# Projections and output projection in two pieces on TensorE, the time step in four, and new places for some tasks

## The chip, the cores and the metric

The kernel runs on one core of one Trainium2 chip. The metric is device microseconds of one execution. The names of the engines in the profile: PE is TensorE's matmul, PEld its weight load, DVE is VectorE, ACT is ScalarE, POOL is GpSimd, SP is SyncE, which issues the DMAs here.

## The reference

A decoder layer on x of shape (16, 256, 512), in three parts, each with a residual and a layer norm:

```
x = layernorm(x + mamba(x))            # selective state space, DI = 1024 channels, 16 states
x = layernorm(x + cross_attn(x, ctx))  # 16 heads of 16; channels and positions change their roles
x = layernorm(x + ffn(x))              # quantized weights (-1, 0, 1) and activations (8 bit)

# mamba
hs, gate = x @ W_in_states.T, x @ W_in_gates.T            # (256, 1024) each
hs = silu(causal_conv4(hs) + conv_b)
dt = softplus(hs @ W_dt.T @ W_dtproj.T + b)               # W_dt: to 128
h[l] = exp(A * dt[l]) * h[l-1] + dt[l] * B[l] * hs[l]     # 16 states for each channel
y = (sum_n h * C + hs * D) * silu(gate)
out = y @ W_out.T
```

## The kernel before

**Stages.** Each of the 16 batches goes through four functions: `prep` (state projection, convolution, time step, B and C, softplus), `scan` (gate projection, recurrence, gated output), `attn` (output projection, first norm, keys, queries, values, scores, second norm) and `ffn`. They don't run one after the other: stages of up to five batches are in flight together.

**Tasks and places.** The functions emit no instructions. They make tasks by `task(t, engine, us, fn, after, take, free)`: `t` is the place, counted in slots, with 32 slots for each batch (NSL); `us` is what the planner takes the task to last; `after` names the tasks that have to be done; `take` and `free` name buffers of rings (`Hold`). At the end `run()` plays all of this through in a planner's time: whenever an engine is idle there, it starts the ready task with the lowest `t`, not more than AHEAD = 12.29 slots past the first task that hasn't begun, and emits its instructions. A task's end is known to others HOP = 0.2 us later, and 0.3 us later where PE did it. So the order on each engine's queue is fixed by the planner, and a task is never interrupted. On the chip each queue runs in that order, with semaphores between the engines.

**Constants.** The places are constants at the head of the file: a batch b starts at T = 32 b; PREP, TSP, BCP, SOFT for `prep`; GATE, SUMP, WEIGHP for `scan`; OUT0 and OUT1 for the two halves of the output projection, KP and QP for keys and queries, NORM for the second norm, FFN, FSTEP, FUP, FDN for the feed-forward part, WS0 and WQ0 for the passes over the feed-forward weights at the start.

**Rings.** Buffers are few. TensorE's results go to PSUM: five banks (`ps`) are shared by projections, scores, sums and the rest; two more hold decays (`dA`) and one the attention output (`av`). There are seven `h` buffers (the states of 32 channels and four state groups), two `z`, two `win`, one `wr` (used in turn by the step weights and by the context), one `wout`, three `xres`.

**The long TensorE tasks.** Each is one task of 3.45 us in the planner:
- `project` (L491): 8 fp32 matmuls, that is two channel tiles of four k steps, into the two halves of a PSUM bank. `prep` makes four of them per batch, `scan` four more (gates). After one in `prep` come ACT (L510), three DVE steps for each half (L517), ACT (L530) and DVE (L520); after one in `scan` ACT (L641) and DVE (L638).
- the time step (L544): 8 matmuls, one chain of accumulation. For batch 0 it is cut in four already.
- the output projection (L736): four matmuls of 512 columns, one chain of accumulation, for each half of the channels and each row tile; then DVE adds to the residual (L740).

**The other TensorE tasks** are short: scores (L830), values (L896), state sums (L694 and L697, 2.45 us in the planner), key and query projection (L763), feed-forward (L1013, L1086), transposes.

**The recurrence.** For each tile d of 128 channels and each of four groups, POOL makes the product dt*hs*B (L233, `h<-bcr,dtr`), ACT the decays (L668), DVE two scans (L672), POOL the product with C (L233, `h<-h,bcr`). Then PE sums over the states (L697) and frees four `h` buffers, and DVE multiplies by the gate (L705). The loads `dtr<-dtd` (L654) feed it.

Of the kernel before, what the change touches and what calls it, by code (L numbers as in the profile page):

```python
# [20 lines left out]
P = 128  # L21
L = 256
# [3 lines left out]
NDT = DI // P  # L26
# [18 lines left out]
SOFT = -7.09  # L45
SSTEP = 9.0
VUNITS = 24
GATE = -0.34
OUT0 = 25.01
OUT1 = 34.11  # L50
PSTEP = 2.02
TSP = 15.44
BCP = 9.29
KP = 34.45
QP = 37.76
VP = -3.68
SUMP = 0.16
WEIGHP = 1.88
FSTEP = 0.74
FUP = -0.18  # L60
BACK = 0.59

SHIFT = [(0, 0, 0, 0, 0, 0)] * 16
# [3 lines left out]
SLAG = 7.79  # L67
GSTEP = 3.93
SCAN = -0.29
NORM = 81.05  # L70
FFN = 98.49
WQ = 3.57
WQ0 = 21.99
WS = 0.66
WS0 = 14.23
AHEAD = 12.29
HOP = 0.2
RINGS = {
# [8 lines left out]
def decoder_kernel(ctx, tc, x, xT, ctx_in, mask, winT, wdtT, wbcT, wdpT, woutT, dvec, wqkvT, bqk, bv, wguT, wdnT, out):  # L87
    nc = tc.nc
# [55 lines left out]
    def task(t, eng, us, fn, after=(), take=(), free=(), kb=0):  # L144
        if any(h.tag == "ps" for h in free) and eng in ("DVE", "ACT"):
            t -= BACK
        k = Task()
        k.t, k.i, k.eng, k.us, k.fn, k.take, k.free, k.kb = t, len(tasks), eng, us, fn, take, free, kb
        k.then, k.begun = [], False
        k.left = len(after)  # L150
        for p in after:
            p.then.append(k)
        for h in take:
            h.first = k
        for h in free:
            h.users += 1
        tasks.append(k)
        return k

    def led(h, *after):  # L160

        return tuple(after) + ((h.first,) if h.first is not None else ())
# [90 lines left out]
    for i in range(RINGS["dA"]):  # L253

        t = ps.tile([P, 2, L], F32, tag=f"dA{i}", name=f"dA{i}", bufs=1)
# [7 lines left out]
    def cut(t, a, b):  # L263
        return t.rearrange("p (a b) -> p a b", a=a, b=b)
# [28 lines left out]
    for g in range(NB4):  # L293
# [7 lines left out]
        for n in range(1, NB4):  # L301
            t = cut(free["tmp"][n % 2][:, : NDT * NS // NB4], NDT, NS // NB4)
# [180 lines left out]
        h = Hold(tag)  # L483
        return h, dma(t, lambda: nc.sync.dma_start(out=cut(h.t, 4, 2 * P), in_=winT[:, :, c0 : c0 + 2 * P]), (), (h,), (), 512)

    def project(ps_t, hx, hw):

        xt, ws = cut(hx.t, 4, L), cut(hw.t, 4, 2 * P)
        for i in range(2):
            for k in range(4):  # L490
                nc.tensor.matmul(ps_t[:, i * L : (i + 1) * L], ws[:, k, i * P : (i + 1) * P], xt[:, k, :], start=k == 0, stop=k == 3)  # L491


    def prep(b):
        st = S[b]
        T = b * NSL + SHIFT[b][0]
        hx, t_x = st["xT"] = load_x(T + PREP - 3, b)
# [6 lines left out]
        for d0 in range(0, NDT, 2):  # L504
            t = T + PREP + PSTEP * d0
            hw, t_w = load_win(t - 5, d0 * P) if b else load_win(T + PREP - 3 + 0.1 * d0, d0 * P, "h")
            pb, z = Hold("ps"), Hold("tmp")

            def first(i, pb=pb, z=z, d0=d0):
                nc.scalar.activation(  # L510
                    z.t[:, i * L : (i + 1) * L], pb.t[:, i * L : (i + 1) * L], AF.Identity, bias=cw[:, d0 + i, 4:5], scale=cw[:, d0 + i, 3:4]
                )

            def conv(i, j, pb=pb, z=z, d0=d0):
                s = 3 - j
                zi = z.t[:, i * L + s : (i + 1) * L]
                nc.vector.scalar_tensor_tensor(zi, pb.t[:, i * L : (i + 1) * L - s], cw[:, d0 + i, j : j + 1], zi, ALU.mult, ALU.add)  # L517

            def silu(pb=pb, z=z, d0=d0):
                nc.vector.scalar_tensor_tensor(u2_of(d0), cut(pb.t, 2, L), 1.0, cut(z.t, 2, L), ALU.add, ALU.mult)  # L520

            uh = (st["u"][d0 // 4],) if d0 % 4 == 0 else ()
            m = task(t, "PE", 3.45, lambda pb=pb, hw=hw: project(pb.t, hx, hw), led(st["u"][d0 // 4], t_x, t_w), (pb, z) + uh, (hx, hw))
            ends = []
            for i in range(2):
                k = task(t, "ACT", 0.52, lambda i=i, f=first: f(i), (m,))
                for j in (2, 1, 0):
                    k = task(t, "DVE", 0.42, lambda i=i, j=j, f=conv: f(i, j), (k,))
                ends.append(k)
            k = task(t, "ACT", 0.53, lambda pb=pb, z=z: nc.scalar.activation(pb.t, z.t, AF.Tanh), tuple(ends))  # L530
            st["t_u"].append(task(t, "DVE", 0.61, silu, (k,), (), (pb, z)))
        U = tuple(st["t_u"])


        t = T + PREP + TSP
        hw, hts, hbc = Hold("wr"), Hold("ts"), Hold("bc")
        hwd = Hold("win" if b else "h")
        t_wdt = dma(t - 3 if b else T + PREP - 2, lambda: nc.sync.dma_start(out=cut(hwd.t, NDT, P), in_=wdtT), (), (hwd,), (), 512)
        t_wdp = dma(t - 1 if b else T + PREP - 1.9, lambda: nc.sync.dma_start(out=hw.t, in_=wdpT), (), (hw,), (), 512)
        pts, p2, p3, hp2 = Hold("ps"), Hold("ps"), Hold("ps"), Hold("o")  # L540

        def time_step(d0, n):
            for d in range(d0, d0 + n):
                nc.tensor.matmul(pts.t[:, :L], cut(hwd.t, NDT, P)[:, d, :], u_of(d), start=d == 0, stop=d == NDT - 1)  # L544
# [12 lines left out]
            src = st["bcd"][o : o + NS, :].rearrange("(n j) l -> n (j l)", n=NB4)  # L557
            nc.sync.dma_start(out=h.t, in_=src[None].broadcast_to([DB, NB4, NS // NB4 * L]))

        if b:  # L560
            m = task(t, "PE", 3.45, lambda: time_step(0, NDT), U + (t_wdt,), (pts, hts), (hwd,))
        else:
            for i in range(4):
                m = task(
                    t, "PE", 0.87, lambda i=i: time_step(2 * i, 2), (U[i], m if i else t_wdt), (pts, hts) if i == 0 else (), (hwd,)
                )
        t_ts = task(t, "ACT", 0.37, lambda: nc.scalar.copy(hts.t, pts.t[:, :L]), (m,), (), (pts,))
        m = task(T + PREP + BCP, "PE", 1.1, bc, U + (t_wbc,), (p2, hbc, hp2))
        m = task(T + PREP + BCP, "ACT", 0.37, lambda: nc.scalar.copy(hp2.t, p2.t[:, :L]), (m,), (), (p2,))
        m = task(T + PREP + BCP, "PE", 0.5, lambda: nc.tensor.matmul(p3.t[:32, :L], sel4, hp2.t, start=True, stop=True), (m,), (p3,), (hp2,))  # L570
        m = task(T + PREP + BCP, "ACT", 0.36, lambda: nc.scalar.copy(hbc.t, p3.t[:32, :L]), (m,), (), (p3,))
        m = dma(t + 0.5, bc_store, (m,), (), (hbc,), 32)
# [6 lines left out]
        for hf in range(2):  # L579
            t = T + SOFT + SSTEP * hf  # L580
# [17 lines left out]
            for i, (d, h) in enumerate(zip(ds, hs)):  # L598
# [10 lines left out]
                m = task(t + 1 + i, "POOL", 1.25, times, (t_s,))  # L609
# [4 lines left out]
    def scan(b):  # L614
        st = S[b]
# [14 lines left out]
        hx, t_x = st["xT"]  # L630
        st["z"], st["t_z"] = [], []
        for i in range(4):
            d0, t = 2 * i, T + 8 * i + GATE
            hw, t_w = load_win(t - 5, DI + d0 * P)
            pb, z = Hold("ps"), Hold("z")

            def silu(pb=pb, z=z):
                nc.vector.scalar_tensor_tensor(z.t, z.t, 1.0, pb.t, ALU.add, ALU.mult)  # L638

            m = task(t, "PE", 3.45, lambda pb=pb, hw=hw: project(pb.t, hx, hw), (t_x, t_w), (pb, z), (hx, hw))  # L640
            m = task(t, "ACT", 0.53, lambda pb=pb, z=z: nc.scalar.activation(z.t, pb.t, AF.Tanh, scale=0.5), (m,))  # L641
            st["z"].append(z)
            st["t_z"].append(task(t, "DVE", 0.61, silu, (m,), (), (pb,)))
        for d in range(NDT):
            hs, ws = [], []
            for g in range(NB4):
                k = NB4 * d + g
                t = T + k - SCAN
# [28 lines left out]
                f = dma(t - 4, fetch, (st["t_dt"][d // 2],), (hd,), (), 256)  # L677
# [10 lines left out]
            pb = Hold("ps")  # L688
# [18 lines left out]
            m = task(T + 4 * d + 4 + SUMP, "PE", 2.45, sums, tuple(ws), (pb,), tuple(hs))  # L707
# [3 lines left out]
    def attn(b):  # L711
        st = S[b]
# [5 lines left out]
        U = T + SHIFT[b][2]  # L718
# [6 lines left out]
        for hf in range(2):  # L725
            hw = Hold("wout")
            wo = lambda hw=hw: cut(hw.t, 4, H)
            t_w = dma(U + (OUT1 if hf else OUT0) - 8, lambda hf=hf, wo=wo: nc.sync.dma_start(out=wo(), in_=woutT[:, 4 * hf : 4 * hf + 4, :]), (), (hw,), (), 1024)
            for lt in range(2):
                t = U + (OUT1 if hf else OUT0) + 0.7 * lt  # L730
                pb = Hold("ps")

                def mult(hf=hf, lt=lt, pb=pb, wo=wo):
                    for i in range(4):
                        u = cut(st["u"][hf].t, 4, L)
                        nc.tensor.matmul(pb.t, u[:, i, lt * P : (lt + 1) * P], wo()[:, i, :], start=i == 0, stop=i == 3)  # L736

                def add(lt=lt, pb=pb):

                    nc.vector.scalar_tensor_tensor(x1()[:, lt, :], pb.t, 0.5, x1()[:, lt, :], ALU.mult, ALU.add)  # L740

                m = task(t, "PE", 3.45, mult, (t_w,) + tuple(st["t_y"][4 * hf : 4 * hf + 4]), (pb,), (hw, st["u"][hf]))
                adds[lt].append(task(t, "DVE", 0.61, add, (m, t_x1), (), (pb,)))
        t_n1 = layernorm(U + OUT1 + 1.3, hr, adds)

# [3 lines left out]
        t = T + OUT1 - 1  # L749
# [43 lines left out]
        for s in range(4):  # L793
            t = T + att + SLAG + VP + 0.7 * s
            pb = Hold("ps")
# [9 lines left out]
            m = task(t, "PE", 1.0, mult, (t_c, t_wqkv, t_bv) + (tuple(S[b - 1]["t_av"]) if b else ()), (pb,), (hc,))  # L805
# [122 lines left out]
        t = T + NORM + SHIFT[b][4]  # L928
# [11 lines left out]
        m = task(t, "DVE", 0.5, lambda: nc.vector.reciprocal(hrc.t, hsm.t), (t_sm,), (hrc,), (hsm,))  # L940
# [236 lines left out]
```

## Time and profile before

| | us |
|---|---|
| runs: median of 3 (lowest, highest) | 3010.79 (3008.86, 3011.28) |
| profiled execution, its own time | 3007.98 |
| its span, first to last instruction | 3005.8 |
| busy: PE, PEld | 2650.5, 1319.4 |
| busy: DVE, ACT, POOL | 2674.1, 2334.0, 2596.5 |
| mean granted TensorE clock | 0.965 |

A line of the groups or of the timeline names the line of the kernel, the engine, the operation and the tiles. Two matmul records stand for one fp32 matmul. In the list of waits, "POOL h L233 <- PE bank L697" says that POOL's instruction of L233 waited for the matmul of L697, with the us in total, the number of times and the longest. A row of the windows gives, for a stretch of time, the busy us of PE, PEld, DVE, ACT and POOL with the number of instructions in brackets, then the granted clock, the share of the DMA engines and GB/s.

### The profile page before, as it was taken

The page shows a single profiled execution, that of the slowest core. Times are in us where ns is not written, and L with a number is a line of the kernel's source. Part 1 is how long each engine was busy: PE and PEld are TensorE (multiplying, and loading weights), DVE is VectorE, ACT ScalarE, POOL GpSimd, SP SyncE. Part 2 cuts the span into 40 slices and gives each one's busy share as a digit, 9 for nine tenths or more (in the row PEclk, how much of TensorE's full clock was granted, in tenths as well). Part 3 has the DMA queues.
Part 4 walks back from the last instruction along what each step waited for, and adds up shares of the span by engine and source line. Part 5 has one row for each costly group of instructions (what it writes and reads, how often), then busy time and mean ns, then how long its engine had stood idle before and what let it go on. Part 6 is the DMA issues. An engine that isn't in the chain of part 4 may idle for free.

```text
span 3005.8 us, 51881 instructions
## 1 busy us (share of the span) xinstructions
PE 2650.5 (88%) x17514; PEld 1319.4 (44%) x17514; DVE 2674.1 (89%) x4043; ACT 2334.0 (78%) x4731; POOL 2596.5 (86%) x1435
## 2 busy tenths in 40 slices
PE   6567888999989999898999989899998999999995
PEld 4333443454545445444444544444353544434333
DVE  6969888999989999898999989899999989999873
ACT  4787978787787878778787877878788787888674
POOL 3899999999898999989899998989989899999311
PEclk9787999999999999999999999999999999999998
DMA  6695776566465665746665574656646566564432
GB/s 215 222 305 182 233 224 205 188 199 206 143 218 182 204 195 171 224 138 214 193 200 186 168 224 150 216 189 196 189 157 226 165 203 193 187 203 147 125 98 71
DMA packets 363250, 567.46 MB, mean 189 GB/s; under 512 B 47316, under 2 KB 200024, under 8 KB 358888
## 3 DMA queue, kind: packets, MB, share of 16 engines
q1 hardware_dynamic: 362984, 564.16, 58.2%
q8 instruction: 137, 2.24, 0.3%
q14 instruction: 129, 1.06, 0.1%
HBM read 449.61 MB, written 114.43 MB: 188 GB/s over the span
## 4 chain that ended last, share of the span: by engine, by line
POOL 28%; PE 27%; DVE 16%; ACT 13%; issue 10%; DMA 5%; SPq 1%; POOLq 0%; ACTq 0%; DVEq 0%
POOL h L233 23%; DVE h L672 7%; PE bank L491 6%; ACT pT L889 4%; PE bank L697 4%; DVE mx L845 4%; PE av L896 3%; PE bank L830 3%; ACT dA L668 3%; PE bank L1013 3%; PE bank L763 2%; PE bank L799 2%; DMA dtr<-dtd 2%; ACT xres L469 1%; POOL s L233 1%
## 5 line engine op out<-in xcount | busy, mean ns | idle before, releaser
L672 DVE TENSOR_TENSOR_SCAN h<-dA,h 128x512 f32<-128x512 f32 x1024 | 1223.3, 1208 | 83.0 <-POOL h L233 41.2
L233 POOL TENSOR_TENSOR h<-h,bcr 128x1024 f32<-128x1024 f32 x512 | 1207.9, 2363 | 95.7 <-DVE h L672 92.9
L233 POOL TENSOR_TENSOR h<-bcr,dtr 128x1024 f32<-128x1024 f32 x500 | 1177.7, 2363 | 69.9 <-PE bank L697 63.4
L668 ACT ACTIVATE dA<-dtr,A 128x255 f32<-128x255 f32 x2048 | 963.9, 475 | 297.1 <-DVE h L672 255.6
L830 PE MATMUL bank<-qk 108*128 108x512 bf16 x2003 | 616.3, 385 | 78.9 <-DVE mx L845 44.7
L845 DVE TENSOR_REDUCE mx<-bank 128x1 f32<-128x512 f32 x1004 | 655.1, 675 | 25.8 <-PE bank L830 25.6
L889 ACT ACTIVATE pT<-bank 128x512 f32<-128x512 f32 x999 | 566.6, 590 | 119.1 <-PE bank L830 113.9
L491 PE MATMUL bank<-xT,win 128*128 128x256 f32 x1984 | 454.5, 382 | 20.4 <-DVE u L520 7.8
L896 PE MATMUL av<-pT,vaug 128*32 128x256 f32 x4096 | 336.2, 397 | 106.6 <-ACT pT L889 104.5
L491 PEld LDWEIGHTS bank<-xT,win 128*128 128x128 f32 x1984 | 377.2, 192 | 83.8 <-DVE u L520 9.5
L830 PEld LDWEIGHTS <-qk 108*128 108x128 bf16 x2048 | 179.7, 98 | 392.2 <-issue 264.2
L697 PE MATMUL bank<-h,sel 128*32 128x256 f32 x4096 | 262.0, 399 | 49.0 <-POOL h L233 48.9
L1013 PE MATMUL bank<-fw,xqT 128*128 128x512 fp8e4 x976 | 248.5, 381 | 12.5 <-DVE hq L1023 4.0
L896 PEld LDWEIGHTS av<-pT,vaug 128*32 128x32 f32 x4096 | 88.8, 109 | 356.8 <-ACT pT L889 277.9
L736 PE MATMUL bank<-wout,u 128*128 128x512 f32 x512 | 231.0, 595 | 4.9 <-DVE u L705 4.4
L697 PEld LDWEIGHTS bank<-h,sel 128*32 128x32 f32 x4096 | 124.1, 114 | 180.9 <-POOL h L233 72.2
L517 DVE SCALAR_TENSOR_TENSOR tmp<-bank,cw,tmp 128x254 f32<-128x254 f32 (+2 forms) x384 | 165.1, 468 | 7.8 <-ACT tmp L510 7.7
L1013 PEld LDWEIGHTS <-xqT 128*128 128x128 bf16 x1024 | 96.3, 98 | 151.4 <-issue 57.6
L736 PEld LDWEIGHTS bank<-wout,u 128*128 128x128 f32 x512 | 96.0, 190 | 108.5 <-issue 94.4
L1086 PE MATMUL bank<-fw,s 128*128 128x512 fp8e4 x496 | 127.0, 380 | 1.8 <-ACT s L1077 1.1
L233 POOL TENSOR_TENSOR s<-s,u 128x512 f32<-128x512 f32 x64 | 80.7, 1272 | 39.9 <-ACT s L595 39.9
L705 DVE TENSOR_TENSOR u<-bank,z 128x256 f32<-128x256 f32 x128 | 52.8, 413 | 60.9 <-PE bank L697 60.8
(157 smaller groups left out, 2961.7 us busy)
## 6 DMA issues: line engine op xcount, KB each, us to landing
dtr<-dtd SPq DMA_DIRECT2D x512, 256.0 KB
win<-in_winT SPq DMA_DIRECT2D x124, 512.0 KB
qk<-sqk SPq DMA_DIRECT2D x128, 384.0 KB
dtd<-s SPq DMA_DIRECT2D x64, 512.0 KB
wout<-in_woutT SPq DMA_DIRECT2D x32, 1024.0 KB
fw<-gu_q SPq DMA_DIRECT2D x64, 512.0 KB
sqk<-qf SPq DMA_DIRECT2D x64, 384.0 KB
bcr<-bcd SPq DMA_DIRECT2D x32, 512.0 KB
```

The source lines that it names most:

```text
L233: return nc.gpsimd.tensor_tensor(out, a, b, ALU.mult)
L491: nc.tensor.matmul(ps_t[:, i * L : (i + 1) * L], ws[:, k, i * P : (i + 1) * P], xt[:, k, :], start=k == 0, stop=k == 3)
L517: nc.vector.scalar_tensor_tensor(zi, pb.t[:, i * L : (i + 1) * L - s], cw[:, d0 + i, j : j + 1], zi, ALU.mult, ALU.add)
L668: nc.scalar.activation(ha.t[:, i, 1:], hd.t[:, 1:L], AF.Exp, scale=A[:, d, g, j : j + 1])
L672: nc.vector.tensor_tensor_scan(seg, ha.t.rearrange("p n l -> p (n l)"), seg, 0.0, ALU.mult, ALU.add)
L697: m = nc.tensor.matmul(pb.t[DB * g : DB * g + DB, :L], sel, cut(hs[g].t, J, L)[:, j, :], start=False, stop=j == J - 1, tile_position=(0, D ...
L736: nc.tensor.matmul(pb.t, u[:, i, lt * P : (lt + 1) * P], wo()[:, i, :], start=i == 0, stop=i == 3)
L830: nc.tensor.matmul(pb.t, qk()[:, j, side, c * P : (c + 1) * P], qk()[:, j, 1 - side, :], start=True, stop=True)
L845: task(t, "DVE", 0.62, lambda pb=pb, c=c, j=j: nc.vector.tensor_reduce(mx()[:, j, c : c + 1], pb.t, AX.X, ALU.max), (m,), (), (pb,))
L889: V["x"] = nc.scalar.activation(hp.t[:, j * H : (j + 1) * H], pb.t, AF.Exp, scale=DSC)
L896: i = nc.tensor.matmul(hav.t[32 * k : 32 * k + 32, :], vaug_f[:, c, c0 : c0 + 32], hp.t[:, j * H + h * L : j * H + (h + 1) * L], start=c == 0,
L1013: nc.tensor.matmul(pb.t, xqT()[:, i, t * P : (t + 1) * P], wu()[:, k, i, :], start=i == 0, stop=i == 3)
```

## The change

`project` makes two tasks of 1.73 us now, one for each channel tile, the second after the first. The output projection becomes two tasks of two matmuls each; the cut lies inside its chain of accumulation. The time step of every batch is cut in four tasks of two matmuls, as it was for batch 0. What follows them waits for the last piece. Nine places are changed.

```diff
-GATE = -0.34
-OUT0 = 25.01
-OUT1 = 34.11
+GATE = -1.46
+OUT0 = 24.55
+OUT1 = 33.92
-BCP = 9.29
-KP = 34.45
+BCP = 9.42
+KP = 33.05
-FSTEP = 0.74
-FUP = -0.18
+FSTEP = 0.66
+FUP = -0.8
-NORM = 81.05
+NORM = 82.79
-WS0 = 14.23
+WS0 = 12.95
...
-    def project(ps_t, hx, hw):
-
-        xt, ws = cut(hx.t, 4, L), cut(hw.t, 4, 2 * P)
-        for i in range(2):
+    def project(t, pb, hx, hw, need, got):
+
+        def mult(i):
+            xt, ws = cut(hx.t, 4, L), cut(hw.t, 4, 2 * P)
             for k in range(4):
-                nc.tensor.matmul(ps_t[:, i * L : (i + 1) * L], ws[:, k, i * P : (i + 1) * P], xt[:, k, :], start=k == 0, stop=k == 3)
+                nc.tensor.matmul(pb.t[:, i * L : (i + 1) * L], ws[:, k, i * P : (i + 1) * P], xt[:, k, :], start=k == 0, stop=k == 3)
+
+        m = task(t, "PE", 1.73, lambda: mult(0), need, got, (hx, hw))
+        return task(t, "PE", 1.73, lambda: mult(1), (m,), (), (hx, hw))
...
-        if b:
-            m = task(t, "PE", 3.45, lambda: time_step(0, NDT), U + (t_wdt,), (pts, hts), (hwd,))
-        else:
-            for i in range(4):
-                m = task(
-                    t, "PE", 0.87, lambda i=i: time_step(2 * i, 2), (U[i], m if i else t_wdt), (pts, hts) if i == 0 else (), (hwd,)
-                )
+        for i in range(4):
+            m = task(
+                t, "PE", 0.87, lambda i=i: time_step(2 * i, 2), (U if b else U[i : i + 1]) + (m if i else t_wdt,), (pts, hts) if i == 0 else (), (hwd,)
+            )
...
-                def mult(hf=hf, lt=lt, pb=pb, wo=wo):
-                    for i in range(4):
+                def mult(i0, hf=hf, lt=lt, pb=pb, wo=wo):
+                    for i in (i0, i0 + 1):
...
-                m = task(t, "PE", 3.45, mult, (t_w,) + tuple(st["t_y"][4 * hf : 4 * hf + 4]), (pb,), (hw, st["u"][hf]))
+                m = task(t, "PE", 1.73, lambda f=mult: f(0), (t_w,) + tuple(st["t_y"][4 * hf : 4 * hf + 4]), (pb,), (hw, st["u"][hf]))
+                m = task(t, "PE", 1.73, lambda f=mult: f(2), (m,), (), (hw, st["u"][hf]))
```

More of the change, by code (lines that the diff above doesn't have):

```diff
@@ L522, in prep @@
             uh = (st["u"][d0 // 4],) if d0 % 4 == 0 else ()
-            m = task(t, "PE", 3.45, lambda pb=pb, hw=hw: project(pb.t, hx, hw), led(st["u"][d0 // 4], t_x, t_w), (pb, z) + uh, (hx, hw))
+            m = project(t, pb, hx, hw, led(st["u"][d0 // 4], t_x, t_w), (pb, z) + uh)
             ends = []
@@ L638, in silu @@
                 nc.vector.scalar_tensor_tensor(z.t, z.t, 1.0, pb.t, ALU.add, ALU.mult)
-            m = task(t, "PE", 3.45, lambda pb=pb, hw=hw: project(pb.t, hx, hw), (t_x, t_w), (pb, z), (hx, hw))
+            m = project(t, pb, hx, hw, (t_x, t_w), (pb, z))
             m = task(t, "ACT", 0.53, lambda pb=pb, z=z: nc.scalar.activation(z.t, pb.t, AF.Tanh, scale=0.5), (m,))
```

## Prediction

> **What bounds the kernel now.** I read the page first: engine shares, then the slices.
>
> ```profile
> PE 2650.5 (88%) x17514; PEld 1319.4 (44%) x17514; DVE 2674.1 (89%) x4043; ACT 2334.0 (78%) x4731; POOL 2596.5 (86%) x1435
> ...
> PE   6567888999989999898999989899998999999995
> ...
> DVE  6969888999989999898999989899999989999873
> ...
> POOL 3899999999898999989899998989989899999311
> ```
>
> Three engines are within 3% of each other, and the slices are flat after the first few. So I looked for the beat: the first gate product (L705) of each batch starts 177.1 to 177.3 us after that of the batch before in seven of the last nine batches. One such beat, by windows:
>
> ```profile
> 2026.80:2203.90 177.10, 162.62 (x1095) 81.53 (x1094) 164.63 (x248) 140.82 (x289) 163.88 (x90) 0.99 0.60 190
> ```
>
> DVE is idle for 12.5 us of it, POOL for 13.2, PE for 14.5. No engine is the floor alone. What can be won is in these waits, listed for the same 177 us (POOL first, then DVE):
>
> ```profile
> POOL h L233 <- DVE h L672: 7.1, 3, 4.8
> POOL h L233 <- PE bank L697: 4.5, 2, 3.5
> ```
>
> ```profile
> DVE u L705 <- PE bank L697: 3.8, 4, 1.7
> DVE h L672 <- POOL h L233: 2.1, 3, 1.0
> ...
> DVE bank L766 <- PE bank L763: 1.1, 1, 1.1
> DVE xres L740 <- PE bank L736: 1.0, 1, 1.0
> ```
>
> The largest wait on PE is POOL's 3.5 us: its next product needs an h buffer that the state sums (L694, L697) free. TensorE's rows just before it:
>
> ```profile
> 2200.67 0.39 PE L830 MATMUL bank<-qk 108*128 108x512 bf16 x1
> 2200.90 3.62 PE L491 MATMUL bank<-xT,win 128*128 128x256 f32 x16
> 2204.35 0.60 PE L830 MATMUL bank<-qk 108*128 108x512 bf16 x2
> 2204.88 0.63 PE L694 MATMUL bank<-u,diag 32*32 32x256 f32 x8
> 2205.45 1.93 PE L697 MATMUL bank<-h,sel 128*32 128x256 f32 x32
> ```
>
> A whole projection (16 records, 3.45 us from its start to the next block's) lies ahead of the sums. POOL's last product before the gap starts at 2201.57 and lasts 2.36, so the sums could have run at 2203.93; L697 starts at 2205.45, 1.5 us late.
>
> Last, the clock. The granted clock is 1.00 in nearly all of the beat, but not here:
>
> ```profile
> 2131.00:2134.00 3.00, 1.86 (x12) 0.47 (x12) 3.00 (x6) 2.34 (x5) 2.85 (x4) 1.00 0.02 5
> 2134.00:2137.00 3.00, 2.25 (x12) 0.87 (x12) 2.81 (x4) 2.97 (x7) 3.00 (x3) 0.86 0.48 165
> 2137.00:2140.00 3.00, 3.00 (x11) 0.56 (x10) 1.91 (x3) 1.97 (x5) 3.00 (x2) 0.57 0.63 179
> ```
>
> Once per beat the clock is at half for 3.4 us, just when the first query projection (L763) runs: 3.54 us where the second takes 1.88. The drop is missing in two beats, and those two last 175.5 us. So this drop is worth 1.7 us of each beat.
>
> **The change, part by part.** A slot of the planner is 177.1 / 32 = 5.53 us. The beat is repeated 12 times (L705 at 550.1 and at 2672.1, 2122 us); the start and the end are costed at no change (bounds 3 us each way: their waits are for loads, softplus and ACT, in no row for a cut block).
>
> *The cuts.* No instruction is added or taken away. Per batch there are 8 projections, 4 output projections (3.45 us each) and one time step; they get 8 + 4 + 3 = 15 cuts. The second piece waits for the first, and in the planner TensorE's result arrives 0.3 us after it falls idle. So at each cut any ready task that may start goes in between.
> - Removed: a wait behind the second half. In the rows above a cut at 2200.90 + 1.73 = 2202.63 comes before 2203.93, when the sums become ready, so the sums don't get in at that cut unless something short (the score pair, 0.53) fills it, and then they save only what the scores no longer take. Bounds 0 and -1.5 us; I take -0.9 (sums straight after the second piece and the scores already done, some 0.5, and 0.4 for a cut that falls better in some batches). The other sums of the beat start on POOL's products or behind a query projection that isn't cut: 0.
> - Added: the second half comes later by what goes in between, 0.6 us (a score pair or a value product). Behind it wait the three convolutions and the gate (under cover of the next batch's lead, 0) and the residual add L740, which waits already 1.0 us per beat. With half of the four output cuts filled and 1.4 such waits a batch (22 in the list of waits of the whole span, over 16 batches): 0.6 x 1.4 / 2 = +0.4. Bounds 0 and +0.8.
> - The switch itself: the next block starts 0.17 us before the end given for L491 (2200.90 + 3.62 = 2204.52 against 2204.35), as inside a block, so 0. Upper bound by PEld's "issue" gaps of 0.41 us: 15 x 0.41 = 6.2 us of TensorE's 14.5 idle, still covered.
>
> The Trainium skill speaks against cuts here: "TensorE: Matmul & The Clock Gate", section "The cost: per-tile semaphore tail", gives 26.3 ns for each more semaphore increment. By it, as an estimate, 15 cuts cost 0.4 us a batch and the sum below would be -10 us instead of -14; no row here shows this price.
>
> *KP* (1.40 slots, 7.7 us earlier): two key projections with 1.72 us on PE each, then per projection three DVE steps (0.74, 0.68, 0.67), two ACT casts (0.58) and three stores on SP. It can't move by all of this: the context load (L750) leaves at 2112.21, when the step weights free its buffer, and the first key matmul runs at 2119.09 behind an output projection that began at 2115.55. With a cut at 2117.3 it goes in there, 1.8 us earlier. DVE idles 0.75 (before 2116.85) and 0.77 (before 2120.75) there, which the key's DVE steps can fill partly: -0.7 (bounds 0 and -1.5). SP's stores go past the dtr loads (L654, 0.52 each), which run four slots ahead: 0.
>
> *GATE* (6.2 us earlier): the win load, PE, one tanh, one DVE step. Order only; the z buffers are two and the load has its own lead of five slots: 0, within the bounds of the d3 stall. *OUT0, OUT1* (2.5 and 1.1 us earlier, with the wout and residual loads): they wait for gates in any case: 0. *NORM* (9.6 us later): four POOL products of 1.28, a reciprocal, nine DMAs on SP; POOL does them without a wait before or after its place, and the FFN comes 15 slots later: 0, bounds 1.2 each way (the 1.17 us waits of POOL on scans). *FSTEP, FUP*: the same 16 DVE steps of 0.67 in 29 us instead of 33, the second product 3.4 us sooner; POOL's 4.8 us wait is for scans behind these: 0, bounds 1.3 each way (two such steps). *BCP, WS0*: start and 0.7 us: 0.
>
> *The clock drop*: 0, bounds 1.7 each way.
>
> Sum of a beat: -0.9 + 0.4 - 0.7 = -1.2; times 12 is -14.4. The profiled execution took 3007.98 (span 3005.8 and 2.2 around it): 2993.6. The median of the runs is 2.8 above it: **2996.4, say 2996**.
>
> **The clock, rule against row.** PE's gaps ahead of the drop are 0.88, 0.82, 0.55 and 0.39 us with PE busy 1.86 of 3.00 us, and yet the clock fell. So on these rows a stretch that is merely thinner can lose it, and moving a key projection (2127.47 now, 1.72 us) out of the time ahead of this stretch can make it longer. The Trainium skill, "TensorE: Matmul & The Clock Gate", section "Why this matters for your kernels", asks only for no idle gap over about 3 us between bursts; by that rule the drop would not be there at all, and the change could not lose more clock. The rows decide: the drop stays a risk.
>
> **Rivals.**
> - *Slower, the clock.* The thin stretch spans a second window of 3.4 us: another 1.7 us per beat, on the chain since the query projections and the sums behind them stand there; cuts gain nothing and cost their 0.4. +2.1 x 12 = +25: 3036. It decides once PE stays near 1.9 of 3.0 us for some 3.4 us more. For it: K leaves that neighbourhood. Against: cut second halves may fill it.
> - *Slower, the context load.* Brought into the cut, K starts 5.1 us after its load's issue (now 6.9 without a wait). Chain pieces of loads half its size take 4.0 to 5.3 us. If it lands at 6.9, PE stands 1.8 us with the output projection's second half and the sums behind: 1.8 x 12 = +22 on the sum, 2993.6 + 22 + 2.8 = 3018. It decides at a landing past 5.1 us.
> - *Faster, the drop goes.* The second halves and the moved gate fill the thin stretch: -1.2 - 1.7 = -2.9 x 12 = -35: 2976. For it: two beats of 175.5 show that it is a near thing.
> - *The cuts do nothing*: planner fills them with tasks that would have run anyway; waits change place. 3011.
>
> **How the numbers follow.** A measurement here tells apart about 0.2% (6 us). Forecast case (2985 to 3004) 0.34, drop gone 0.22, nothing 0.10, clock worse 0.19, load 0.12, other losses 0.03. Faster 0.56, same 0.10, slower 0.34. The bounds all added give -1.5 - 1.5 - 1.7 = -4.7 a beat, -56, 2954; the clock rival at its 3036 is the end above, with a little for orders that I can't foresee: 2956 to 3038. The faster cases alone hold 2956 to 3004.
>
> **What would show it.** Right: L491 in runs of 8 records; POOL's waits on L697 under 3.6 us a beat; a beat near 175.9; L740's wait near 1.4. Wrong: two half-clock windows a beat; a wait of L763 on the context load; a beat over 177.3; or a gain that stands in the start or the end, where I cost nothing.

## The result, and the profile after

| | before | after |
|---|---|---|
| median of the runs, us (lowest to highest; seven runs each) | 3010.79 (3008.86 to 3011.81) | 3018.12 (3014.02 to 3022.97) |
| profiled execution, its span | 3005.8 | 3016.3 |
| first gate product (L705) of batch 0 starts at | 74.4 | 80.1 |
| mean of the last twelve beats (batch 3 to batch 15) | 176.83 | 177.15 |
| from the first gate product of batch 15 to the end | 333.8 | 334.9 |
| mean granted clock | 0.965 | 0.964 |

The change makes the kernel slower: 1.0026 of the time before, 95% interval 1.0015 to 1.0038, 7.3 us between the medians. The forecast was 2996, faster. The two spans differ by 10.5 us, mostly since the profiled execution of before was 2.8 faster than its median. The three rows in the middle split these 10.5: 5.8 are lost before the first gate product, nothing between it and batch 3 (-0.2), 3.8 over the twelve beats, 1.1 at the end.

The page after, in the lines that I read first before:

```profile
PE 2662.4 (88%) x17514; PEld 1313.2 (44%) x17514; DVE 2673.0 (89%) x4043; ACT 2332.1 (77%) x4733; POOL 2598.0 (86%) x1435
...
PE   5567998999999999899999989999998999999995
...
DVE  5869898998989899898989989898998989999863
```

The same work in the same number of matmuls, DVE and POOL instructions. PE is busy 12 us longer with them. ACT has two instructions more, which turn up below.

One beat of after by windows (columns as before: us, then the busy us of PE, PEld, DVE, ACT and POOL, then the clock):

```profile
1972.10:2149.70 177.60, 163.17 (x1096) 81.03 (x1095) 164.32 (x249) 140.31 (x290) 164.01 (x91) 0.99 0.60 191
```

The waits in the same stretch, first POOL's:

```profile
POOL h L233 <- DVE h L672: 8.3, 3, 3.9
POOL qf L953 <- ACT hq L1064: 2.5, 1, 2.5
POOL h L233 <- PE bank L697: 1.2, 1, 1.2
```

The stall that I aimed at did shrink, from 4.5 to 1.2 us a beat. Yet POOL's listed waits sum to 12.0 us against 11.6 before: the time came back as waits for the scans (L672) and for ACT. DVE's waits:

```profile
DVE u L705 <- PE bank L697: 3.8, 3, 3.0
DVE h L672 <- ACT dA L668: 2.9, 3, 1.9
DVE h L672 <- POOL h L233: 2.1, 2, 1.8
...
DVE xres L740 <- PE bank L736: 0.4, 1, 0.4
```

The wait of L705 has one piece of 3.0 us now (longest 1.7 before). TensorE's timeline shows what it waits for (start, duration, then what PE waited for in brackets):

```profile
2099.43 1.89 PE L491 MATMUL bank<-xT,win 128*128 128x256 f32 x8
2101.45 0.64 PE L897 MATMUL av<-pT,vaug 128*32 128x256 f32 x8
2102.02 0.63 PE L694 MATMUL bank<-u,diag 32*32 32x256 f32 x8
2105.52 3.42 PE L697 MATMUL bank<-h,sel 128*32 128x256 f32 x32 [2.87 <-POOL h L233]
```

The projection runs in pieces of eight records now. The sums of one channel tile (d = 6) get to TensorE before POOL's product is ready, PE stands for 2.87 us, and then L697 takes 3.42 us instead of 1.93. Windows of the same place:

```profile
2102.00:2105.00 3.00, 0.66 (x12) 0.15 (x8) 1.80 (x2) 1.30 (x4) 3.00 (x2) 1.00 0.93 328
2105.00:2108.00 3.00, 2.48 (x24) 1.18 (x28) 1.11 (x2) 1.40 (x3) 2.79 (x2) 0.53 0.81 253
```

The half-clock stretch of before, at the first query projection, is gone; there is one here instead. Of the last twelve beats of before ten hold such stretches, of after ten as well; nine of before's eleven stretches cover the query projection, nine of after's ten these sums. The drop moved.

### The profile page after: what moved, and what is told of

Read it like the earlier page. It is cut to its first block, busy times and chain, and to the rows that moved or that the text cites. A ratio compares the mean times of both kernels' runs of the same rounds, so it can differ in the third digit from the quotient of the medians.

```text
span 3016.3 us, 51889 instructions
## 1 busy us (share of the span) xinstructions
PE 2662.4 (88%) x17514; PEld 1313.2 (44%) x17514; DVE 2673.0 (89%) x4043; ACT 2332.1 (77%) x4733; POOL 2598.0 (86%) x1435
## 4 chain that ended last, share of the span: by engine, by line
PE 25%; DVE 25%; POOL 18%; ACT 13%; issue 10%; DMA 9%; SPq 1%; POOLq 0%; ACTq 0%; DVEq 0%
POOL h L233 14%; DVE h L672 10%; PE bank L491 5%; DVE mx L846 5%; ACT pT L890 4%; PE bank L831 4%; PE bank L697 4%; PE av L897 4%; ACT dA L668 3%; DVE tmp L520 2%; DMA qk<-sqk 2%; PE bank L800 2%; DMA dtr<-dtd 2%; PE bank L736 2%; DVE hq L1026 1%
## 5 line engine op out<-in xcount | busy, mean ns | idle before, releaser
L672 DVE TENSOR_TENSOR_SCAN h<-dA,h 128x512 f32<-128x512 f32 x1024 | 1222.6, 1207 | 83.0 <-ACT dA L668 49.6
L491 PE MATMUL bank<-xT,win 128*128 128x256 f32 x1984 | 484.1, 388 | 28.1 <-DVE u L523 17.7
L491 PEld LDWEIGHTS bank<-xT,win 128*128 128x128 f32 x1984 | 375.9, 193 | 128.7 <-issue 22.8
L897 PE MATMUL av<-pT,vaug 128*32 128x256 f32 x4096 | 329.4, 393 | 79.2 <-ACT pT L890 74.9
L697 PE MATMUL bank<-h,sel 128*32 128x256 f32 x4096 | 271.6, 410 | 59.7 <-POOL h L233 59.5
L736 PE MATMUL bank<-wout,u 128*128 128x512 f32 x512 | 240.9, 596 | 1.2 <-DVE u L705 0.4
L697 PEld LDWEIGHTS bank<-h,sel 128*32 128x32 f32 x4096 | 126.7, 116 | 193.7 <-POOL h L233 86.1
L520 DVE SCALAR_TENSOR_TENSOR tmp<-bank,cw,tmp 128x255 f32<-128x255 f32 (+2 forms) x384 | 164.1, 471 | 12.3 <-ACT tmp L513 12.1
L469 ACT ACTIVATE xres<-xres,lnb,lrs 128x512 f32<-128x512 f32 x96 | 73.9, 806 | 46.6 <-POOL lnb L466 46.3
```

The costliest lines, as they stand in the source:

```text
L491: nc.tensor.matmul(pb.t[:, i * L : (i + 1) * L], ws[:, k, i * P : (i + 1) * P], xt[:, k, :], start=k == 0, stop=k == 3)
L672: nc.vector.tensor_tensor_scan(seg, ha.t.rearrange("p n l -> p (n l)"), seg, 0.0, ALU.mult, ALU.add)
L697: m = nc.tensor.matmul(pb.t[DB * g : DB * g + DB, :L], sel, cut(hs[g].t, J, L)[:, j, :], start=False, stop=j == J - 1, tile_position=(0, D ...
L897: i = nc.tensor.matmul(hav.t[32 * k : 32 * k + 32, :], vaug_f[:, c, c0 : c0 + 32], hp.t[:, j * H + h * L : j * H + (h + 1) * L], start=c == 0,
```

## The experiments

My theory had two parts: the start is lost by the new places, and in the beat the half-clock stretch was only moved, so that what the cuts won is not seen. The rivals: the cuts themselves cost time, at the start or in the beat; or the moved keys wait for their context load. The kernel before ran again beside each experiment and had medians of 3009.8 to 3010.9.

### Cuts and places apart

Cuts with eight of the nine places as before (OUT0 alone is new):

```diff
 # after, with before's places:
-GATE = -1.46, OUT1 = 33.92, BCP = 9.42, KP = 33.05, FSTEP = 0.66, FUP = -0.8, NORM = 82.79, WS0 = 12.95
+GATE = -0.34, OUT1 = 34.11, BCP = 9.29, KP = 34.45, FSTEP = 0.74, FUP = -0.18, NORM = 81.05, WS0 = 14.23
```

> All cuts of the change with the places of before, OUT0 alone at its new 24.55 (the planner finds no order with all nine old places and the cuts). Theory A (the loss stands in the start and is made by the new places, above all GATE with its earlier win load): the first gate product at 74 to 76 us as before, a beat near 177, time 3006 to 3012. Theory B (the cuts make the loss, in the start too): first gate product at 79 to 81 us, time 3015 to 3020. Theory C (nothing but the clock's phase in the first 20 us): no relation, time between both, and the half-clock stretch at the start ends 3 us later in the runs with a late start.

Measured 3063.62, ratio 1.0175 (1.016 to 1.019), far above all expected times. The first gate product comes at 75.6, the mean beat is 181.3, with 19 half-clock stretches in the last twelve beats. So the cuts don't lose the start.

The control for that one place:

```diff
 # before:
-OUT0 = 25.01
+OUT0 = 24.55
```

> The kernel before with OUT0 alone at 24.55: the control for the run with the cuts at old places. Every theory expects little: first gate product near 74.4 us, time within 5 us of before. What it differs by is the size of what one place that moves by 2.5 us does by itself.

Measured 3012.32, 1.0001 (0.999 to 1.0011), first gate product at 75.6: this place alone is worth nothing that can be told.

The other half, before's code without a cut and with eight of the new places (KP stays at 34.45):

```diff
 # before, with after's places:
-GATE = -0.34, OUT0 = 25.01, OUT1 = 34.11, BCP = 9.29, FSTEP = 0.74, FUP = -0.18, NORM = 81.05, WS0 = 14.23
+GATE = -1.46, OUT0 = 24.55, OUT1 = 33.92, BCP = 9.42, FSTEP = 0.66, FUP = -0.8, NORM = 82.79, WS0 = 12.95
```

> No cuts, eight of the nine new places (KP stays at 34.45, since the planner finds no order for all nine). Theory A (places): first gate product near 80 us, time 3015 to 3020. Theory B (cuts): first gate product near 74.4 us, time 3006 to 3012.

Measured 3043.33, 1.0109 (1.0088 to 1.013), again far above the expected times, first gate product at 80.3, mean beat 178.8. The start is lost with the places even where nothing is cut. And cuts and places can't be priced one by one: either half alone (but for one place each) costs over 32 us, both together 7.

One place of after taken back:

```diff
 # after:
-KP = 33.05
+KP = 34.45
```

> The kernel after with KP alone back at 34.45: the control for the run without cuts at the new places, and the price of KP by itself. Theories A and B: the start as in after (first gate product near 80 us), time 3013 to 3021. If my rival of the context load held (key projection early, TensorE waiting for the load), this one would be faster than after by up to 22 us: 2996.

Measured 3026.92, 1.0054 (1.0041 to 1.0067), mean beat 177.93. The moved keys help by 8.8 us against after, some 0.7 a beat, so they don't wait for their load to any loss (in after TensorE's waits for the context load sum to 9.0 us over the span, in before to 11.2). But the last twelve beats hold 17 half-clock stretches instead of 10, and 7 x 1.7 = 12 us is more than the difference: this isn't the filled DVE idle that I had in mind.

### The start

The gate of batch 0 at its old place:

```diff
 # after, in scan:
-            d0, t = 2 * i, T + 8 * i + GATE
+            d0, t = 2 * i, T + 8 * i + (GATE if b else -0.34)
```

> After, but GATE for batch 0 alone at its old -0.34 (project, tanh and win load of the first batch's gates, so the next win load goes behind the first four dtr loads on SP's queue again). Theory A (the start's loss is made by GATE: in after a win load that waits for TensorE stands ahead of the first dtr loads): first gate product at 75 to 76 us, 4 to 5 us sooner than after, beats unchanged near 177.3, time 3012 to 3014. Theory B (the cuts make the start late): first gate product stays near 80 us, time near 3018.

Measured 3018.63, 1.0028 (1.0016 to 1.004), first gate product at 77.5, neither as theory A expected. Half of the start came back, the total didn't move. So I tried the places from the other side, in the kernel before:

```diff
 # before:
-WS0 = 14.23
+WS0 = 12.95
 # and in scan:
-            d0, t = 2 * i, T + 8 * i + GATE
+            d0, t = 2 * i, T + 8 * i + (GATE if b else -1.46)
```

> The kernel before with two of the nine places new where they act on the start: GATE = -1.46 for batch 0 alone, WS0 = 12.95 (the pass over the feed-forward weights). No cut. Theory 'the start is lost by these two places': the first gate product comes at 79 to 81 us instead of 74.4, the beat stays at 176.8, the time is 3014 to 3017. Rival 'it needs the other places or the cuts': first gate at 74 to 77, time 3008 to 3013.

Measured 3016.86, 1.0027 (1.0016 to 1.0039); first gate product at 80.6, mean beat 176.83 and end 333.9 as before. With no cut in the program, two places acting on the start alone cost as much as the whole change.

GATE moves three things together: the load of the gate's weights on SP (`win`, L484, five slots ahead of the gate), the gate's matmuls, and its tanh on ACT. SP's timeline shows the load. Before (start, duration; L607 stores what the softplus and POOL made, L654 loads `dtr`, L361 are small copies of 16 KB):

```profile
42.19 0.40 SPq L607 DMA_DIRECT2D dtd<-s  x1
42.68 3.77 SPq L361 DMA_DIRECT2D mrow<-tmp  x7
46.55 0.38 SPq L607 DMA_DIRECT2D dtd<-s  x1
46.97 2.68 SPq L654 DMA_DIRECT2D dtr<-dtd  x4
```

The same in this experiment:

```profile
43.51 3.79 SPq L361 DMA_DIRECT2D mrow<-tmp  x7
47.39 0.57 SPq L484 DMA_DIRECT2D win<-in_winT  x1
48.06 0.56 SPq L607 DMA_DIRECT2D dtd<-s  x1
48.68 3.28 SPq L654 DMA_DIRECT2D dtr<-dtd  x4
```

A `win` load of 512 KB now stands ahead of the first `dtr` loads (256 KB each). POOL's first h product, before and here, waits for the first of these:

```profile
50.74 4.66 POOL L233 TENSOR_TENSOR h<-bcr,dtr 128x1024 f32<-128x1024 f32 x2 [4.87 <-DMA dtr<-dtd]
54.04 4.66 POOL L233 TENSOR_TENSOR h<-bcr,dtr 128x1024 f32<-128x1024 f32 x2 [2.54 <-DMA dtr<-dtd]
```

It starts 3.8 us after the load's issue before, 5.4 us after it here. In after it is the same: `win` at 47.67, the first `dtr` load at 48.96, POOL's product at 54.26 behind a wait of 2.32 for it. The sixteen profiles of this study fall into three groups (us):

| GATE of batch 0, WS0 | profiles | first `dtr` load issued to POOL's first h product | that product to the first gate product | first softplus to the first gate product |
|---|---|---|---|---|
| both old (WS0 14.0 in two) | 6 | 3.1 to 3.8 | 23.1 to 23.7 | 33.9 to 35.2 |
| WS0 alone new | 3 | 3.2 to 3.5 | 24.0 to 25.1 | 34.3 to 37.2 |
| both new | 7 | 5.3 to 5.6 | 25.8 to 27.0 | 39.6 to 41.6 |

In the seven, and in none of the nine, a `win` load stands between the first store of L607 and the first `dtr` loads. Behind POOL's product another 2 to 3 us are lost: the critical chain of after waits 7.29 us for a `dtr` load issued at 62.27, just after the next `win` load (61.6) and the first loads for the pass over the feed-forward weights (60.9 on). No run moved a load without its tanh, or the gate without WS0, so that the loads do it is read from the traces and not tested by itself.

ACT's order changes too, and two instructions more on its page tempt one to blame it. In after (L595 is the softplus, L641 the tanh of a gate):

```profile
38.47 1.70 ACT L595 ACTIVATE s<-bank,dtb 128x256 f32<-128x256 f32 x4 [1.13 <-PE bank L588]
40.19 1.28 ACT L641 ACT_TABLE_LOAD   x1
41.49 0.60 ACT L641 ACTIVATE z<-bank 128x512 f32<-128x512 f32 x1
...
46.62 0.60 ACT L641 ACTIVATE z<-bank 128x512 f32<-128x512 f32 x1 [1.24 <-PE bank L491]
47.23 1.28 ACT L595 ACT_TABLE_LOAD   x1
48.53 1.57 ACT L595 ACTIVATE s<-bank,dtb 128x256 f32<-128x256 f32 x4
```

Two tanh stand between the halves of the softplus, and ACT loads a table for them and another to go back, 1.28 us each. Before, the second half begins at 43.70 with no tanh between. But the same two loads are in the repaired kernel below, with one tanh between:

```profile
40.15 1.28 ACT L641 ACT_TABLE_LOAD   x1
...
43.59 1.28 ACT L595 ACT_TABLE_LOAD   x1
44.89 0.84 ACT L595 ACTIVATE s<-bank,dtb 128x256 f32<-128x256 f32 x2
```

It too has the two instructions more (4733 against 4731), and its first gate product comes at 73.6. So the table loads aren't what the first gate product waits for. Nor does the recurrence begin with the second half: the first two channel tiles need only the first store, and after's first `dtr` loads are issued 0.4 us after its second half has begun.

WS0 alone:

```diff
 # before:
-WS0 = 14.23
+WS0 = 12.95
```

> The kernel before with WS0 = 12.95 alone. If the half of the start that the gate of batch 0 didn't explain (2.6 us) is the weights' pass: first gate at 76.5 to 78, time near 3013. If the gate of batch 0 is needed with it: first gate at 74 to 75.5, time near 3011.

Measured 3007.05, 0.9993 (0.9984 to 1.0003), first gate product at 75.1: the pass over the weights doesn't do it without the gate. The gate without it wasn't run in the kernel before.

Then the repair, both places back in the kernel after (WS0 to 14.0, near the old 14.23):

```diff
 # after:
-WS0 = 12.95
+WS0 = 14.0
 # and in scan:
-            d0, t = 2 * i, T + 8 * i + GATE
+            d0, t = 2 * i, T + 8 * i + (GATE if b else -0.34)
```

> The kernel after with the gate of batch 0 at -0.34 and WS0 = 14.0 (the old 14.23 is 1.3 us later). Theory 'the start is lost by these two places together': first gate product at 74 to 76 us, beat as after (176.8 to 177.2), time 3010 to 3014. Rival 'a place or a cut that isn't named loses the rest': first gate at 77 to 78 as with the gate alone, time 3016 to 3020.

Measured 3004.81, 0.999 (0.998 to 0.9999), better than expected; first gate product at 73.6, mean beat 176.9. 13 us less than after, and 5 under the kernel before that ran beside it: with the two places back the change is a small gain. By the two profiles 6.5 us come back at the first gate product, 5.2 over the first three batches, where the pass over the weights runs (batch 3 starts its gates at 543.9 instead of 555.7), and 3.0 over the beats. The 5.2 aren't sure: with both repairs (below) batch 3 starts at 554.0. Why the gate alone gave nothing in the total isn't settled: its first softplus began at 41.2 us, 2.7 later than in after, and such shifts occur between profiles of programs that start alike (38.5 in after, 40.4 in the run with repeated matmuls below).

### The clock

To hold the clock, TensorE repeats cheap matmuls ahead of the gap. In after the four diagonal matmuls of d = 6 are issued four times, the first three overwritten:

```diff
-                for g in range(NB4):
+                for w in range(4 if d == 6 else 1):
+                    for g in range(NB4):
...
-start=True, stop=False
+start=True, stop=d == 6 and w < 3
```

> After, with the four diagonal matmuls of d = 6 (L694) issued four times, the first three to be overwritten; order and plan of all else as in after. In after TensorE waits 2.9 us there for POOL each beat and then has the clock at half for 3.4 us (L697 3.42 instead of 1.93 us). Theory D (the beat of either kernel is 175.5 plus one half-clock stretch of 1.7 us, which the change has only moved from the query projection to these sums): no half-clock stretch per beat, beat 175.4 to 175.9, time 3018 less 12 times 1.6 = 2998 to 3001. Rival (the drop is harmless since POOL and DVE have slack, the beat is set elsewhere): drop gone, beat still 177.2, time 3016 to 3020, or up to 7 us more if the repeats stand in the way.

Measured 3000.91, 0.9966 (0.9953 to 0.9979), as theory D said: 17 us less than after, for 12 matmuls (24 records) more a batch. TensorE around the place that was slow, in this kernel (its L695 is L694 of after, L698 is L697):

```profile
2092.72 1.89 PE L491 MATMUL bank<-xT,win 128*128 128x256 f32 x8
2094.74 0.64 PE L898 MATMUL av<-pT,vaug 128*32 128x256 f32 x8
2095.31 1.93 PE L695 MATMUL bank<-u,diag 32*32 32x256 f32 x32
2098.80 1.94 PE L698 MATMUL bank<-h,sel 128*32 128x256 f32 x32 [1.56 <-POOL h L233]
```

The sums take 1.94 us, not 3.42. Not one of the last twelve beats holds a half-clock stretch, and their mean is 175.5. POOL's waits in the beat from 1965.89 on:

```profile
POOL h L233 <- DVE h L672: 8.0, 3, 3.7
POOL qf L954 <- ACT hq L1065: 2.4, 1, 2.4
```

The wait on the sums is gone altogether. The same with the gate of batch 0 at its old place (both edits as above):

> Both together. Theories A and D: the gains add, first gate product near 75.5 us and beat near 175.6: 2994 to 2997. If A fails: as after_warm; if D fails: 3012 to 3014.

Measured 3005.93, 0.9984 (0.9975 to 0.9992), first gate product at 77.8, mean beat 175.5. The gains don't add: the start is 3.4 us earlier than with the clock held alone, but batch 3 starts only 1.4 earlier, and the total is 5 us longer. This is as open as the gate alone.

The kernel before, each score matmul between the second key projection and the first query projection of a batch issued twice, the second writing the same values again (`thin[0]` is set behind the one and cleared at the other):

```diff
-                nc.tensor.matmul(pb.t, qk()[...], qk()[...], start=True, stop=True)
+                for _ in range(2 if thin[0] else 1):
+                    nc.tensor.matmul(pb.t, qk()[...], qk()[...], start=True, stop=True)
```

> Before, with each score matmul between the second key projection and the first query projection of a batch issued twice, some six per beat, 1.3 us more of TensorE's work in the thin stretch; nothing else changed. Theory D: the half-clock stretch at the query projection goes, beat 175.5, time 3010.8 less 10 times 1.7 = 2992 to 2996. Rival (harmless drop): 3010 to 3018. If 1.3 us isn't enough to hold the clock, the stretch stays and the beat is 177 to 178: 3010 to 3020, and nothing is said on D.

Measured 3004.72, 0.9987 (0.9974 to 0.9999), between what theory D and its rival expected; mean beat 176.1, one half-clock stretch in the last twelve beats. 151 matmul records more, some 9 a batch. The first query projection takes what the second does:

```profile
2126.93 1.98 PE L766 MATMUL bank<-xres,wqkv 128*128 128x512 f32 x4
...
2133.02 1.88 PE L766 MATMUL bank<-xres,wqkv 128*128 128x512 f32 x4
```

and yet POOL's waits keep the stall on the sums:

```profile
POOL h L233 <- DVE h L673: 7.2, 3, 4.8
POOL h L233 <- PE bank L698: 3.5, 1, 3.5
```

These sum to 10.7 us in a beat; in after with the clock held it was 8.0 + 2.4 = 10.4. So with the clock held in both, the cuts and places together win 176.1 - 175.5 = 0.6 us a beat by the profiles. It may be less: the doubled scores lie on TensorE too, and the two beats of before that lost no clock took 175.5 already. It may be more: this profile (2998.4) is the fastest of its twelve runs, 6 us under their median.

Both repairs, the start's and the clock's:

> The same with the four matmuls of L694 for d = 6 issued four times, as in the run that held the clock. Theory: beat 175.5 and first gate at 74 to 76 add up, 3001 less 5: 2994 to 2998. Rival 'the start's gain is lost on the way to the first full beat': 3000 to 3006, as with the gate's place alone.

Measured 2997.6, 0.9961 (0.9947 to 0.9975), first gate product at 76.0, mean beat 175.45. The fastest of all: 12 us under the kernel before that ran beside it, 20 under after, and 7 under the kernel before with its clock held.

### Which cuts

The output projection whole again in after:

```diff
-                m = task(t, "PE", 1.73, lambda f=mult: f(0), (t_w,) + ..., (pb,), (hw, st["u"][hf]))
-                m = task(t, "PE", 1.73, lambda f=mult: f(2), (m,), (), (hw, st["u"][hf]))
+                m = task(t, "PE", 3.45, lambda f=mult: (f(0), f(2)), (t_w,) + ..., (pb,), (hw, st["u"][hf]))
```

> The kernel after with the output projection whole again (cuts in the projections and the time step stay, all places new). Theory 'the cuts of the projections carry the order that the new places were set for': beat 176.5 to 178, time 3010 to 3025, L740's wait back near 1.0 or less a beat. Rival 'each kind of cut is needed': beat over 178, time over 3030. If my term for L740 (0.4 us a beat) is a real loss: 3013 or less.

Measured 3038.6, 1.0099 (1.0077 to 1.012), the time of the rival "each kind of cut is needed"; mean beat 177.7, from the last batch's first gate product to the end 341.4 (334.9 in after). The waits of the residual add sum to 26.0 us over the span, against 8.8 in after and 21.5 in before.

All projections whole again in after (one task of 3.45 us in place of the two in `project`):

> The kernel after with all eight projections of a batch whole again (cuts in the output projection and the time step stay, all places new). Theory 'the projections' cuts carry it': beat 178.5 to 179.5, time 3035 to 3045, near the 3043.3 of no cut at all; POOL's wait on the sums (L697) back over 3 us a beat. Rival 'each kind carries a part': 3022 to 3034.

Measured 3015.79, 1.0018 (1.0008 to 1.0029): as after, 3018.12, or a little less, and under both expected times. POOL's wait on the sums is back, here with line 699 for 697, and still the mean beat is 177.0:

```profile
POOL h L233 <- DVE h L674: 8.0, 5, 3.1
POOL h L233 <- PE bank L699: 3.7, 3, 2.1
```

There are five half-clock stretches in its last twelve beats, ten in after's. By these two profiles, what the cut projections take from POOL's stall they lose on the clock. And the output cuts, which I had charged with a loss, carry some 20 us at these places.

## Why the prediction was wrong

Two steps failed. The start, at no change, turned the sign: with its two places back the kernel is 13 us faster and under before. The sum of a beat, -1.2, gave too much: the beat became 0.3 longer, in part because the clock drop, priced at 0, moved. With both repaired the time is 2997.6, next to the forecast of 2996, but by luck: the forecast left the drop in, and the run took it out.

**What bounds the kernel**: right. Three engines with 163 to 165 us each in a beat of 177, and what one wait gives, another takes.

**Start and end at no change (3 us each way)**: measured 5.8 us late at the first gate product, and the two places by themselves made the kernel before as slow as after. I priced GATE as a load, a projection, a tanh and a DVE step, "order only", with a lead of five slots for the load; WS0 as "start", with no price. I didn't ask what the moved load would stand ahead of. In the traces it stands ahead of the first `dtr` loads, which the whole recurrence waits for, and the first of them is used 5.3 us after its issue instead of 3.8. That the queue order is the cause, and what WS0 adds, is read from the sixteen profiles; no run separates it.

A table load behind a moved tanh looks like another cause. The Trainium skill, "ScalarE: Activation LUTs", section "Rules for kernel authors", advises to do all the functions of one table set before switching. Its section "What ACT_TABLE_LOAD costs" gives 2.66 us for a switch, a load of 1283 ns and a drain; here the next activation starts 0.02 us after the load of 1.28 ends, so a switch costs 1.3. Two such switches are in the repaired kernel as well, whose start isn't late.

**Cuts, -0.9 a beat for the stall**: the stall fell by 3.3 us as its mechanism said, the beat with the clock held by some 0.6 for all of the change. The term took a wait that goes for time won. POOL's sum of waits stayed (11.6 and 12.0).

**Residual add, +0.4**: wrong in sign. L740's wait was 0.4, not 1.4, and whole output projections cost 20 us.

**KP, -0.7**: about right in size (0.7 a beat by taking it back), not in kind: the half-clock stretches changed with it. The rival that K would wait for its load falls.

**The clock at 0, bounds 1.7 each way**: within the bounds, but priced wrongly. The drop left the query projection, as my "drop goes" rival said, and came back at the sums of d = 6. Held, the beat of after is shorter by 177.15 - 175.5 = 1.65 us, that of before by 176.83 - 176.1 = 0.7. Taken at its word, the drop costs 0.9 more in after, which with the -0.6 is the +0.3 measured. But both kernels have drops in ten of twelve beats, and the doubled scores may cost before some of what they win, so how the 0.3 splits stays open. The Trainium skill's rule that I weighed against the row ("TensorE: Matmul & The Clock Gate", section "Why this matters for your kernels") wants no idle gap over about 3 us. A gap of 2.87 stood ahead of the drop in after, none over 0.88 in before: the clock fell in both.

**Semaphore price of a cut**: the skill's 0.4 us a batch can't be seen beside these moves; no run here shows it.

**The other places and the range**: OUT1, BCP, FSTEP, FUP and NORM were not moved one by one, so their zeros are untested. And the bounds "all added" leave out the 1.2 of NORM, the 1.3 of FSTEP and the 3 us each of start and end.

**What would show it**: runs of 8 for L491 and the wait on L697 came as said; the beat near 175.9 didn't, "a beat over 177.3" showed in five of the last nine. And the doubt that I noted was the true one with the sign turned: the loss that turned the sign stands in the start, "where I cost nothing".

## What to carry to other kernels

When a step is moved and its load moves with it, look at what the load then stands ahead of on the queue of loads, above all at the start, where one chain feeds everything. Before a new instruction in a slow trace is blamed, look for it in a fast one: here the two table loads more are in both. A stall that a cut removes counts only after asking what is late next: here the waits of the stalled engine had the same sum before and after. And where a clock drop comes once per beat, hold the clock first and then compare orders; else each order is judged by where its drop happens to fall.

## Not expected of the hardware

- Work that computes nothing made the kernel faster. Twelve repeated matmuls a batch kept the granted clock at 1.00 over the last twelve beats and won 17 us of 3018.
- No single gap decides a drop here. The clock fell behind a stretch with PE busy 1.86 of 3.00 us and no gap over 0.88 us (before), and held through windows with 2.87 and 1.44 of 3.00 busy and a gap of 1.56 us (after, repeated matmuls).
- Half clock comes on a fixed grid. In each of the sixteen profiles all half-clock stretches start at whole multiples of 3.413 us from each other. Between 500 and 2700 us, a step of that grid at full clock was always followed by half clock where PE was busy in it, by its records, for under 1.4 us, and never where it was busy for over 2.15. A beat of 177.15 is a little short of 52 steps (177.5), so the same thin place falls on other parts of the grid from beat to beat; this may be why some beats keep their clock.
- The time from the program's start to the first softplus differs by up to 4.4 us between profiles (38.2 to 42.6), partly among programs that begin alike, and sets a limit to what the start can be read to.
